# Local attention of an adaLN block: head scores in a two-bank PSUM tile, mask by a product, one maximum, exponentials from PSUM, norms for two chunks at once

## Chip, cores and metric

The kernel runs on one core of one Trainium2 chip. The time is device microseconds (us) of one launch; lower is better. TensorE is called PE, VectorE DVE, ScalarE ACT, GpSimd POOL, and the queue that issues most transfers SP. L965 means line 965 of the kernel before, whose functions are printed below with their line numbers.

## The reference, cut to what matters

The input is x of 16 batches, 512 tokens, 128 features. An attention with latent keys and values (16 heads of 8) comes first, wrapped in adaLN modulation. Then two layers follow, each with a windowed ("local") attention of 8 heads of 64 and a gated MLP. The change touches the local attention:

```
q, k, v = split(shift(x) @ wqkv)                 # 8 heads of 64
q = l2norm(q) * qs ;  k = l2norm(k) * ksc
q, k = rotary_xpos(q, k)
# windows of 64 queries, each against its own 64 keys and the 64 keys before them
sim  = einsum(q * 8, k)
mask = (i < j) | (i > j + 64) | (j == -1)
sim  = where(mask, -max, sim)
out  = einsum(softmax(sim), v)
x    = x + out @ wo
```

## The kernel before

The first attention fills about the first 700 us. Each of the two layers then has a local-attention part (about 715 to 1270 us and 1455 to 2050 us in the profiled execution) and an MLP part after it.

The local attention works in chunks of 128 tokens, that is two windows of 64; there are 4 chunks in each of 16 batches and 2 layers, so 128 chunks. `proj_steps` makes q, k and v of a chunk, `chunk_steps` does its attention, and `out_steps` multiplies by wo once in a batch.

- Projection, `blk(n)`: for each of q, k, v three 512-column matmuls (L877 to L879: high and low parts of the operands) into one PSUM bank `ps_s`. For q and k, ACT squares the bank (L887), DVE multiplies it twice with the rotary tables (L891), DVE sums the squares (L901), POOL adds the two products into `r` (L904). `norm` takes the inverse square root of the 16 sums (L916, two small ACT instructions, L189, L192, L195), stores minus 8 times that of q in `nrq` (L921) and multiplies k by its own on POOL (L923). `tr(j)` transposes r with four PE instructions (L930) and ACT copies the result to qT or kT (L143).
- Scores, `s1(par)`: four heads of one parity (even or odd; they lie in partitions 0-63 or 64-127) go into one bank `ps_e` (L965, a 64x64 piece of the array each). Then for each of the four heads one DVE instruction (L978) adds the mask, multiplies by `nrq`, writes `pr` to SBUF and yields the minimum; one ACT instruction for each head takes the exponential of `pr` and its sum `den` (L161).
- `nrm(par)` divides by the sum (DVE L1005, POOL L1006), `s2(par)` transposes (L1014) and copies to pT (L143), `s3` multiplies by v (L1034), ACT rounds the result to `oh` (L143), DVE keeps the rest in `ol` (L1046). `out_steps` is L817 to L819 and L1066.

The order is not that of the loops. A `Plan` gives every step a due time (`LQ` for the six projection steps, `LC` for the eight steps of a chunk, `UC` the length of a chunk) and emits the steps sorted by it; the compiler then schedules the emitted instructions with a timeline of its own. Each engine runs its list in order.

PSUM has eight banks. In the layers the kernel uses three for `ps_s`, two for `ps_e`, two for `ps_m` and one `ps_x`, which every third request of `third("m")` or `third("e")` takes: transposes, the product with v and the product with wo thus turn through three banks. `FB` sets the number of SBUF buffers of hh, hl, sq, t1, t2, r, pr, pT. The MLP part (`mlp_steps`) uses `ps_s` for its gate and up products and `third("e")` for its two transposes.

## Time and profile before

| | |
|---|---|
| median of 3 runs | 2212.19 us (2210.29 to 2213.22) |
| profiled execution, own time | 2217.06 us |
| its span, first to last instruction | 2215.3 us |
| PE busy | 2019.9 us, 91% |
| DVE busy | 1915.9 us, 86% |
| ACT busy | 1622.7 us, 73% |
| POOL busy | 1234.0 us, 56% |
| mean granted TensorE clock | 0.953 |

The profiled execution took 0.22% longer than the median of the runs. Busy time of an engine is the union of its instructions; matmuls are pipelined and overlap, so the sum of their durations is far above the time PE needs for them, and the distance from one start to the next is the better price. "Idle before" is the time for which the engine stood still ahead of an instruction, with the engine whose result ended the wait.

### The profile page before, as it was taken

The page shows a single profiled execution, that of the slowest core. Times are in us where ns is not written, and L with a number is a line of the kernel's source. Part 1 is how long each engine was busy: PE and PEld are TensorE (multiplying, and loading weights), DVE is VectorE, ACT ScalarE, POOL GpSimd, SP SyncE. Part 2 cuts the span into 40 slices and gives each one's busy share as a digit, 9 for nine tenths or more (in the row PEclk, how much of TensorE's full clock was granted, in tenths as well). Part 3 has the DMA queues.
Part 4 walks back from the last instruction along what each step waited for, and adds up shares of the span by engine and source line. Part 5 has one row for each costly group of instructions (what it writes and reads, how often), then busy time and mean ns, then how long its engine had stood idle before and what let it go on. Part 6 is the DMA issues. An engine that isn't in the chain of part 4 may idle for free.

```text
span 2215.3 us, 55787 instructions
## 1 busy us (share of the span) xinstructions
PE 2019.9 (91%) x20362; PEld 1359.0 (61%) x20362; DVE 1915.9 (86%) x5869; ACT 1622.7 (73%) x4318; POOL 1234.0 (56%) x1500
## 2 busy tenths in 40 slices
PE   5879898989985999999999998889999999999888
PEld 3334444444433777777777766667777777777665
DVE  6767788878855999999999999999899989898898
ACT  2666777777784888888888755577788888887555
POOL 4345455545554766666666644476566666664334
PEclk7788999999996999999999999999899999999999
DMA  4335544454532110111111100020101011111022
GB/s 125 104 120 151 144 137 141 141 148 136 149 87 56 28 35 18 35 25 29 30 23 35 39 11 1 1 41 21 35 19 32 21 25 28 25 28 23 17 56 76
DMA packets 101198, 132.78 MB, mean 60 GB/s; under 512 B 15538, under 2 KB 77500, under 8 KB 98876
## 3 DMA queue, kind: packets, MB, share of 16 engines
q1 hardware_dynamic: 100444, 128.67, 21.8%
q8 instruction: 161, 2.64, 0.5%
q14 instruction: 113, 0.93, 0.1%
q10 hardware_dynamic: 480, 0.54, 0.1%
HBM read 48.43 MB, written 50.86 MB: 45 GB/s over the span
## 4 chain that ended last, share of the span: by engine, by line
PE 47%; DVE 34%; DMA 10%; ACT 4%; issue 3%; SPq 1%; POOL 1%; DVEq 0%; ACTq 0%; POOLq 0%
PE ps_e L965 9%; DVE t L891 5%; PE ps_m L724 4%; DVE pr L978 4%; PE ps_s L877 4%; DMA kst<-kdd 3%; DVE mx L585 3%; PE ps_m L1014 3%; PE ps_m L1034 3%; DVE ss L901 3%; PE ps_s L878 2%; PE ps_s L879 2%; DMA kdd<-kd 2%; PE ps_m L930 2%; DVE pr L1140 2%
## 5 line engine op out<-in xcount | busy, mean ns | idle before, releaser
L585 DVE TENSOR_REDUCE mx<-ps_w 128x2 f32<-128x1024 f32 (+3 forms) x448 | 390.1, 911 | 97.5 <-PE ps_w L575 94.5
L161 ACT ACTIVATE pr<-pr,m 128x128 f32<-128x128 f32 x1024 | 404.0, 402 | 60.1 <-DVE m L978 57.5
L904 POOL TENSOR_TENSOR r<-t,t 128x512 f32<-128x512 f32 x256 | 328.3, 1283 | 195.7 <-DVE t L891 79.4
L1006 POOL TENSOR_TENSOR pr<-pr,den 128x512 f32<-128x512 f32 x256 | 266.9, 1043 | 211.6 <-DVE den L1005 120.2
L161 ACT ACTIVATE pt<-ps_w 128x1024 f32<-128x1024 f32 x320 | 324.3, 1025 | 69.0 <-PE ps_w L664 64.6
L965 PE MATMUL ps_e<-kT,qT 64*64 64x128 f32 (+1 forms) x4608 | 354.6, 272 | 3.6 <-DVE m L978 1.6
L891 DVE TENSOR_TENSOR t<-ps_s,tab 128x512 f32<-128x512 f32 x512 | 328.4, 678 | 16.2 <-ACT sq L887 8.3
L978 DVE CUSTOM_DVE_ANT_0 pr<-ps_e,maskl,nrq 128x128 f32<-128x128 f32 x1024 | 298.7, 341 | 48.2 <-PE ps_e L965 47.6
L965 PEld LDWEIGHTS ps_e<-kT,qT 64*64 64x64 f32 x4608 | 251.5, 135 | 127.3 <-issue 103.6
L675 POOL TENSOR_SCALAR_AFFINE_SELECT pt<-pt 128x256 f32<-128x256 f32 (+1 forms) x448 | 191.5, 442 | 242.5 <-ACT pt L161 237.8
L724 PE MATMUL ps_m<-pt,vau 128*32 128x512 f32 (+3 forms) x2048 | 204.6, 467 | 13.0 <-ACT o L143 12.9
L1145 POOL TENSOR_TENSOR kT<-pr,qT 128x512 fp32r<-128x512 f32 x96 | 123.0, 1290 | 165.9 <-ACT qT L143 157.5
L877 PE MATMUL ps_s<-wqh,hh 128*128 128x512 f32 x384 | 186.9, 487 | 25.3 <-DVE t L891 18.5
L161 ACT ACTIVATION_READ_ACCUMULATOR pr<-pr,m 128x1 f32 x1024 | 201.7, 197 | 0.0
L887 ACT ACTIVATE sq<-ps_s 128x512 f32<-128x512 f32 x256 | 152.5, 597 | 51.1 <-PE ps_s L879 40.5
L565 PE MATMUL ps_w<-kst,qst 48*128 48x512 bf16 (+3 forms) x1024 | 157.7, 315 | 33.2 <-ACT pt L161 11.4
L901 DVE TENSOR_REDUCE ss<-sq 128x8 f32<-128x512 f32 x256 | 171.3, 673 | 0.3 <-ACT sq L887 0.3
L664 PE MATMUL ps_w<-qst,kst 50*128 50x512 bf16 (+3 forms) x1024 | 131.1, 308 | 31.5 <-DVE mx L585 29.6
L878 PE MATMUL ps_s<-wql,hh 128*128 128x512 f32 x384 | 157.0, 409 | 0.0
L879 PE MATMUL ps_s<-wqh,hl 128*128 128x512 f32 x384 | 155.4, 406 | 0.0
L923 POOL TENSOR_TENSOR r<-r,rky 128x512 f32<-128x512 f32 x128 | 133.7, 1045 | 37.3 <-DVE rky L195 30.0
L575 PEld LDWEIGHTS <-idm 64*128 64x128 bf16 x2048 | 107.4, 99 | 65.7 <-issue 35.1
(215 smaller groups left out, 4521.3 us busy)
## 6 DMA issues: line engine op xcount, KB each, us to landing
od<-o SPq DMA_DIRECT2D x64, 256.0 KB
v<-v SPq DMA_DIRECT2D x32, 512.0 KB
qst<-qdd SPq DMA_DIRECT2D x64, 192.0 KB
kst<-kdd SPq DMA_DIRECT2D x64, 192.0 KB
v<-v SPq DMA_DIRECT2D x32, 384.0 KB
qdd<-qd SPq DMA_DIRECT2D x16, 384.0 KB
kdd<-kd SPq DMA_DIRECT2D x16, 384.0 KB
xt<-in_L_attn_x_dram SPq DMA_DIRECT2D x16, 256.0 KB
```

The lines of the kernel that those rows point to most:

```text
L161: ins = nc.scalar.activation(*a, **k)
L585: nc.vector.tensor_reduce(dst, src, AX.X, ALU.max)
L724: mm_ = nc.tensor.matmul(p[32 * hl : 32 * hl + 32, kb * 128 : T], lhsT=va[:, kb, h * 9 : h * 9 + 32], rhs=pts[hl, seg][:, off : off + n], ...
L877: nc.tensor.matmul(p, lhsT=hh[:, cols], rhs=wqh[:, wc], start=True, stop=False)
L878: nc.tensor.matmul(p, lhsT=hh[:, cols], rhs=wql[:, wc], start=False, stop=False)
L879: nc.tensor.matmul(p, lhsT=hl[:, cols], rhs=wqh[:, wc], start=False, stop=True)
L891: nc.vector.tensor_tensor(t, pv, W["tab"][:, n, 2 * j + k, :].unsqueeze(1).to_broadcast([128, LH, LD]), ALU.mult,)
L901: nc.vector.tensor_reduce(loc["ss"][:, j, :], sq, AX.X, ALU.add)
L904: nc.gpsimd.tensor_tensor(r.rearrange("p h (x d) -> p h x d", x=2), t1.rearrange("p h (x d) -> p h x d", x=2), t2.rearrange("p h (x d) -> ...
L965: nc.tensor.matmul(p[64 * w : 64 * w + 64, hp * 128 + o : hp * 128 + o + n], lhsT=s["q"][r0 : r0 + 64, hp, q0 + 64 * w : q0 + 64 * w + 64] ...
L978: nc.vector.tensor_tensor_reduce(pr[:, hp, :], p[:, hp * 128 : (hp + 1) * 128], mk, s["nrq"][:, cc, 2 * hp + par : 2 * hp + par + 1], 3.0e ...
L1006: nc.gpsimd.tensor_tensor(pr, pr, den.unsqueeze(2).to_broadcast([128, 4, 128]), ALU.mult)
```

## The change

- `s1` becomes one step for all eight heads. It takes a tile of two banks (`two_later`, tag e, two such tiles), one bank for each parity. Four matmuls first write the mask into it, each in its own 64x64 piece of the array: an identity block times a mask tile that is now four heads wide. The score matmuls accumulate onto that and go round the four pieces (two windows, two parities).
- One DVE `tensor_reduce` takes the maximum of all eight heads from PSUM. POOL multiplies it by `nrq` to `nb`. The exponentials (`ex(par)`) read PSUM, with scale `rq` and bias `nb`.
- The projection works on pairs of chunks: `norm` runs once for two chunks, POOL makes `nrq` from `rq`, k is scaled in two steps `kn`, and q is transposed ahead of the norm.
- Banks: `ps_s` two instead of three, `ps_e` two double banks, `ps_m` two, and no `ps_x`. `third` is gone: its users take `ps_m`, in the MLP `ps_s`; gate and up share a double bank. `FB` gives r six buffers instead of four and pr four instead of six.

```diff
-LQ = (0.0, 0.33, 0.26, 0.563, 1.705, 1.964)
-LC = (0.149, 0.637, 0.789, 0.944, 1.14, 1.772, 2.3, 2.531)
+LQ = (0.0, 0.33, 0.26, 1.2)
+LN = (0.6, 0.7, 0.9, 1.6, 1.9)
+LC = (0.149, 0.6, 0.85, 0.944, 1.14, 1.5, 1.85, 2.3, 2.531)
...
-FB = (3, 2, 2, 2, 3, 4, 6, 4)
-BK = (3, 2, 2)
+FB = (3, 2, 2, 2, 3, 6, 4, 4)
+BK = (2, 2, 2)
...
-    def third(tag):
-
-        turn[tag] = (turn.get(tag, -1) + 1) % 3
-        return bank("x", 1) if turn[tag] == 2 else bank(tag, BK[1] if tag == "e" else BK[2])
+    def two_later():
+        return later["ps"].tile([128, 2, 512], F32, tag="e", bufs=BK[1], name="ps_e")
...
-        m = const.tile([128, 128], BF, name=f"maskl{int(first)}")
+        m = const.tile([128, 4, 128], BF, name=f"maskl{int(first)}")
...
             def norm():
                 ss = loc["ss"]
                 nc.vector.tensor_scalar(ss, ss, 1.0e-24, None, ALU.max)
-                rk, nwt = rsqrt_steps(pool["wk"], ss, [128, 2, LH], "rk", nc.vector)
+                rk, nwt = rsqrt_steps(pool["wk"], ss, [128, 2, 2, LH], "rk", nc.vector)
                 for f in nwt:
                     f()
-                nc.vector.tensor_scalar(s["nrq"][:, n, :], rk[:, 0, :], -QKS, None, ALU.mult)
-                r = loc["r", 1]
-                nc.gpsimd.tensor_tensor(r, r, rk[:, 1, :].unsqueeze(2).to_broadcast([128, LH, LD]), ALU.mult)
+                nc.vector.tensor_scalar(
+                    s["rq"][:, n0 : n0 + 2].rearrange("p n r h -> p n h r"),
+                    rk[:, :, 0, :].rearrange("p n (h r) -> p n h r", r=2),
+                    QKS, None, ALU.mult,
+                )
+                nc.gpsimd.tensor_scalar(
+                    s["nrq"][:, n0 : n0 + 2], s["rq"][:, n0 : n0 + 2], -1.0, None, ALU.mult
+                )
+                loc["rk"] = rk
+            def kn(n):
+                def f():
+                    r = loc["r", n, 1]
+                    nc.gpsimd.tensor_tensor(
+                        r, r, loc["rk"][:, n - n0, 1, :].unsqueeze(2).to_broadcast([128, LH, LD]), ALU.mult
+                    )
...
-            return [mm(0), mm(1), mm(2), norm, tr(0), tr(1)]
+            steps = []
+            for n in (n0, n0 + 1):
+                steps += [mm(n, 0), mm(n, 1), mm(n, 2), tr(n, 0)]
+            return steps + [norm, kn(n0), kn(n0 + 1), tr(n0, 1), tr(n0 + 1, 1)]
...
-        def s1(par):
+        def s1():
+            p = loc["s"] = two_later()
+            tiles = [(w, par) for w in range(2) for par in range(2)]
+            for w, par in tiles:
+                r0 = 64 * par
+                nc.tensor.matmul(
+                    p[64 * w : 64 * w + 64, par, :],
+                    lhsT=identb[r0 : r0 + 64, r0 : r0 + 64],
+                    rhs=masks[int(cc == 0 and w == 0)][r0 : r0 + 64].rearrange("p h k -> p (h k)"),
+                    start=True, stop=False, skip_group_check=True,
+                )
+            for hp in range(4):
+                for w, par in tiles:
+                    r0 = 64 * par
+                    k0 = q0 + 64 * w - 64
+                    parts = [(0, k0, 128)] if k0 >= 0 else [(0, 0, 64), (64, 0, 64)]
+                    for o, kk, n in parts:
+                        nc.tensor.matmul(
+                            p[64 * w : 64 * w + 64, par, hp * 128 + o : hp * 128 + o + n],
+                            lhsT=s["q"][r0 : r0 + 64, hp, q0 + 64 * w : q0 + 64 * w + 64],
+                            rhs=s["k"][r0 : r0 + 64, hp, kk : kk + n],
+                            start=False, stop=True, skip_group_check=True,
+                        )
+            m = small("m", [128, 2, 4], 3)
+            nc.vector.tensor_reduce(m, p.rearrange("p r (h k) -> p r h k", h=4), AX.X, ALU.max)
+            nb = loc["nb"] = small("nb", [128, 2, 4], 3)
+            nc.gpsimd.tensor_tensor(nb, m, s["nrq"][:, cc], ALU.mult)
+            loc["den"] = small("den", [128, 2, 4], 3)
+        def ex(par):
             def f():
...
-                for hp in range(4):
-
-                    nc.vector.tensor_tensor_reduce(
-                        pr[:, hp, :],
-                        p[:, hp * 128 : (hp + 1) * 128],
-                        mk,
-                        s["nrq"][:, cc, 2 * hp + par : 2 * hp + par + 1],
-                        3.0e38,
-                        ALU.add,
-                        ALU.min,
-                        m[:, hp : hp + 1],
-                    )
+                pr = loc[par] = flat("pr").rearrange("p (h k) -> p h k", h=4)
                 for hp in range(4):
                     act(
                         "exp",
                         pr[:, hp, :],
-                        pr[:, hp, :],
+                        loc["s"][:, par, hp * 128 : (hp + 1) * 128],
                         AF.Exp,
-                        scale=-1.0,
-                        bias=m[:, hp : hp + 1],
-                        accum_out=den[:, hp : hp + 1],
+                        scale=s["rq"][:, cc, par, hp : hp + 1],
+                        bias=loc["nb"][:, par, hp : hp + 1],
+                        accum_out=loc["den"][:, par, hp : hp + 1],
                     )
...
         def f1():
-            p = third("e")
+            p = ps_s()
...
         def gate(i):
             def f():
                 zh, zl = s["zT"]
-                p = ps_s()
+                s["gu"] = two_later()
+                p = s["gu"][:, 0, :]
...
         def up(i):
             def f():
                 zh, zl = s["zT"]
-                p = ps_s()
+                p = s["gu"][:, 1, :]
```

## The prediction, made before the changed kernel ran

> **What bounds the kernel now.** I read the busy rows over the span first, then the table by stretches, the chain of waits, and at last the order of PE's instructions.
>
> ```profile
> PE   5879898989985999999999998889999999999888
> DVE  6767788878855999999999999999899989898898
> ...
> 900.00:1250.00 350.00, 345.47 (x3762) 262.79 (x3761) 339.40 (x1194) 298.14 (x1032) 230.03 (x205) 1.00 0.13 30
> 1600.00:1950.00 350.00, 350.00 (x3550) 254.78 (x3550) 316.21 (x1116) 287.78 (x960) 218.28 (x194) 1.00 0.13 27
> 1300.00:1430.00 130.00, 117.43 (x559) 83.33 (x558) 125.95 (x372) 65.90 (x109) 62.30 (x52) 1.00 0.02 5
> 2100.00:2190.00 90.00, 79.50 (x363) 58.45 (x363) 88.89 (x278) 53.86 (x86) 35.45 (x28) 0.98 0.20 56
> ```
>
> Columns of the table: stretch, length, busy PE, weight loads, DVE, ACT, POOL, then granted clock and DMA. The first two stretches are the local attention of layers 1 and 2, the last two the MLPs. PE is never idle in layer 2 and 1% idle in layer 1, where DVE too is at 97%. The MLPs are DVE's (97 and 99%). The clock is full, so it decides nothing. A chunk has four L891 instructions; the stretches hold 156 and 150, so a chunk takes 350/39 = 8.97 us in layer 1 and 350/37.5 = 9.33 us in layer 2.
>
> What PE does with that time is seen in starts, not in durations:
>
> ```profile
> 902.78 1.09 PE L965 MATMUL ps_e<-kT,qT 64*64 64x128 f32 x16
> 903.80 0.45 PE L1034 MATMUL ps_x<-pT,v 128*64 128x64 f32 x6
> ...
> 914.93 0.66 PE L1014 MATMUL ps_m<-ident,pr 128*128 128x128 f32 x4
> 915.35 0.48 PE L877 MATMUL ps_s<-wqh,hh 128*128 128x512 f32 x1
> ...
> 916.13 0.40 PE L877 MATMUL ps_s<-wqh,hh 128*128 128x512 f32 x1
> 916.36 0.40 PE L878 MATMUL ps_s<-wql,hh 128*128 128x512 f32 x1
> ...
> 1203.88 1.59 PE L965 MATMUL ps_e<-kT,qT 64*64 64x128 f32 x32
> 1205.40 0.50 PE L877 MATMUL ps_s<-wqh,hh 128*128 128x512 f32 x1
> ```
>
> A 512-column matmul takes 0.23 us from start to start, four transposes 0.42. A score step of 16 takes 1.02; one of 4 takes 0.37 elsewhere, so 0.054 each plus the change of shape. Price of a chunk: nine projection matmuls 2.08, transposes of q and k 0.84, of pr 0.84, 32 of L1034 0.93 (1.08 us for 32 with a change), the share of wo 0.69, scores 1.75 (28 of 128 columns at 0.054, 8 of 64 at half): 7.13 us. In the instruction order I count changes between the three shapes (128x128, 64x64, 128x64): 8.27 a chunk in layer 1, 10.1 in layer 2. (8.97 - 7.13)/8.27 and (9.33 - 7.13)/10.1 both give 0.22 us a change. So both layers are PE's, and layer 2 is slower because its order changes shape more often.
>
> **The change on PE.** Inside one L965 step only the two windows alternate: two pieces of the array. In the run of 32 at 1203.88 both parities meet, and it takes 1.52 us where two steps apart take 2.04. The middle of it shows why:
>
> ```profile
> 1203.95:1204.37 0.42, 0.42 (x9) 1.00 0.00 0
> 1204.46:1204.72 0.26, 0.26 (x16) 1.00 0.00 0
> ```
>
> Each count is of instructions in flight, so it stands over the stretch plus one length (0.27 us): 13 and 30 per us. Four pieces run at about twice the rate of two. The changed step goes round all four, so I price a score instruction at 0.027: 0.87 us a chunk, 0.88 less. The added mask matmuls are four of 512 bf16 columns. The nearest row, L565 with 512 columns, is busy 56.9 us in 256, 0.22 each: 0.92 us one after another, 0.3 with their loads if the four pieces run together. I take 0.3, since the scores show four pieces together; the other end costs 0.62 x 128 = 79 us. The base becomes 7.13 - 0.88 + 0.30 = 6.55. In the order of the changed kernel there are 7.34 and 7.77 shape changes a chunk: 1.61 and 1.71. PE needs 8.16 and 8.26 us a chunk: 0.81 and 1.07 less, times 64, is 52 + 68 = 120 us. This holds only if PE never waits.
>
> **The other engines, a chunk.** DVE has 8.70 us busy in layer 1 (339.4/39). L978 goes: 91.65/39 = 2.35. The maximum comes: 1.22, from the row of L585 over 1024 elements of PSUM. The five small norm instructions (83.2 us in the stretch, 2.13) run half as often: -1.07. Left 6.5. ACT has 7.64. The eight exponentials read PSUM; a 512-column copy takes 584 ns from PSUM and 620 from SBUF, so 0.04 each, 0.29; the two norm instructions (0.43) halve: left 7.1. Here the Trainium skill says more ("VectorE: DVE Perf Modes", section on the TRN2 errata): ScalarE pays 172 cycles plus the columns from PSUM, that is 250 ns here, against 402 in the row of L161, which would take 1.2 us off ACT. But that page's SBUF price, 293 ns, already misses the row by 109, so I keep the difference of the rows; the page's would make my allowance for waits below some 0.2 us a chunk smaller, 26 us off the sum. POOL has 5.90 and gets `nb` and half an `nrq` (0.225 each, the nearest row is L626): 6.2. None reaches PE's 8.2; DVE's 2.2 us fewer are worth nothing by themselves, as PE hides them in both layers.
>
> **What the change makes wait.** Banks. `ps_s` goes from three to two, and everything in `ps_m` from three to two. PE waits in order, so a bank that is late holds up whatever follows. With the prices above I sum PE's work in the changed order between the last projection matmul into a bank and the next one into it. Before, the mean is 8.3 us; after, behind a q or k tile, 4.6, a quarter of them under 3.4. What a tile needs: 0.4 for the matmul's end, 0.6 for the square, 1.26 for the two products, some 2.4 with nothing in front of ACT or DVE. In the trace before it may take 4.9:
>
> ```profile
> 902.46 0.39 PE L879 MATMUL ps_s<-wqh,hl 128*128 128x512 f32 x1
> 903.38 0.59 ACT L887 ACTIVATE sq<-ps_s 128x512 f32<-128x512 f32 x1
> 906.11 1.28 DVE L891 TENSOR_TENSOR t<-ps_s,tab 128x512 f32<-128x512 f32 x2
> ```
>
> Summing the shortfall over all 256 such tiles: 43 us if a tile is held for 3.2 us, 103 for 4.0, 160 for 4.4, 244 for 4.9. DVE has more room than before, which shortens it; ACT is at 87% of PE's new period. I take about 3.6 us, and add nothing for `ps_m`, as a wait for one bank covers that for another: 64 us, 0.5 a chunk. Bounds: nothing, and 160.
>
> The rule that speaks against the change is the Trainium skill's "TensorEngine Tiling (Array Packing)", section PSUM Bottleneck: tiles speed up TensorE, not the emptying of PSUM, so the copies may become the bound. Read strictly, with the engines that empty PSUM at their old pace and tiles held as above (4.4), the gain turns into +40 us; by the rows alone it is -120. I stand between, since DVE, which does empty these banks, loses a quarter of its load.
>
> **New waits.** The exponentials wait for `nb`, and `nb` stands in POOL's queue behind a division (L1006, 1.04 us) that waits for the sums of the chunk before. Between the two groups of exponentials ACT has three to five copies of 0.55 us: 1.7 to 2.8 us, against 0.17 + 1.04 + 0.23 plus hand-overs, about 1.7. Covered, barely; without the cover the ACT queue, and the double bank, wait up to 1 us. The two `kn` steps now lie together, 2.1 us of POOL ahead of the next `r`, which frees t1 and t2 for DVE; DVE's new room covers it.
>
> **At nothing.** The larger mask tiles: eight selects and two memsets grow about fourfold, some 3 us at 21 to 25 us on POOL, whose next instruction there waits 8.4 us for ACT. The first attention: the instructions come in the same order. The MLPs: DVE sets them; the two transposes share two banks, but between the end of one normalisation and the next statistics DVE has about 6 us of other work against 0.8 for transposing. SP's transfers are the same ones. If the MLP cover were gone, 0.8 x 32 = 26 us.
>
> **The sum.** 2217 - 120 + 64 = 2161 us for the profiled execution. That one ran 4.9 us above the median of the runs, so 2156.
>
> **The rivals.**
> - *PE's saving arrives in full* (0.15): the banks come free in time. For it: almost no wait of PE on ACT or DVE in the stretches before. Against: those had three banks. 2217 - 120 - 4.9 = 2092.
> - *The two-bank queue decides* (0.25, slower). The place: the first projection matmul of each tile, waiting for DVE's L891. It cancels the gain from a hold of 4.2 us on (0.94 us of waits a chunk). At 4.4 it gives +40: 2252; at 4.9, +124. For it: the hold of 4.9 shown, and PE's in-order waits. Against: tiles were held long because three banks let them be.
> - *The mask matmuls run one after another* (0.08): 79 us back, 2235.
> - *The four pieces don't run together for the scores either*: 0.88 x 128 = 113 us of the 120 are gone, and with the waits it is slower; the stretch of 16 in 0.26 us speaks against it, and I count it within the second rival.
>
> **How the numbers follow.** My case, a chunk at 8.6 to 8.8 us, has 0.52. The measurement tells about 0.2% (4.4 us) from no change. Faster by more: 0.52 + 0.15 less 0.01, 0.66; within it 0.05, from the edges of my case and of the second rival; slower 0.25 + 0.08 less 0.04, 0.29. The range reaches from a little below PE's full saving, 2085, to the second rival's first price, 2250; its worse holds stay outside, some 0.1, and less than 0.1 lies below.
>
> **What would show it.** Right: the score lines on PE start about 0.03 us apart and the mask lines add under 0.4 us a chunk; DVE falls to about 75% in the layers; PE's idle time ahead of the projection matmul shows DVE L891, about 0.5 us a chunk; a chunk takes 8.6 to 8.8 us in both layers; MLP stretches are unchanged. Wrong: PE waits over 0.9 us a chunk, ACT is the engine at 95%, the mask lines take 0.9 us, or the MLPs grow by more than 10 us.

## The result: slower, 2238 us

| | before | after |
|---|---|---|
| median | 2211.24 us (2207.09 to 2213.22, 4 runs) | 2238.21 us (2236.22 to 2241.32, 4 runs) |
| ratio, 95% interval | | 1.0126, 1.0107 to 1.0145 |
| span of the profiled execution | 2215.3 us | 2235.7 us |
| layer 1, a chunk, from the first batch's end to the last one's | 8.87 us | 9.17 us |
| layer 2, the same | 9.30 us | 9.18 us |

The last two rows count 60 chunks between the last addition of `out_steps` (L1089 after) in batch 1 and in batch 16: after, 786.8 to 1336.7 us in layer 1, 1548.1 to 2098.6 in layer 2. The 20.4 us of span lie so: 5.1 up to the first batch of layer 1, 17.7 in layer 1, 2.0 in the MLP between the layers, -7.3 in layer 2, 2.9 behind it.

The forecast was 2156 us, 56 us faster than before; the kernel is 27 us slower. That lies inside the range, but it comes about in another way than any that I gave.

The page of the profile after, PE and DVE in 40 slices, and the table by stretches (length, busy PE, weight loads, DVE, ACT, POOL, clock, DMA):

```profile
PE   5878899989984898988888888778888888988887
DVE  6767888787855687777777889977777778788897
```

```profile
900.00:1250.00 350.00, 311.83 (x3808) 228.09 (x3806) 270.39 (x498) 302.05 (x960) 239.03 (x260) 1.00 0.13 27
1600.00:1950.00 350.00, 312.35 (x3806) 228.14 (x3801) 265.58 (x488) 303.42 (x964) 233.67 (x257) 1.00 0.12 25
1320.00:1450.00 130.00, 105.98 (x462) 75.06 (x461) 124.28 (x345) 58.87 (x96) 56.95 (x47) 1.00 0.02 5
2120.00:2210.00 90.00, 79.29 (x359) 55.48 (x359) 88.29 (x267) 53.08 (x85) 35.79 (x28) 1.00 0.19 53
```

The nines of PE in the layers are now eights: PE is idle for 38 us of 350, 11%, where it was idle for 1% in layer 1 and never in layer 2 before. DVE has fallen to 77 and 76%, ACT stands at 86%, no engine is full. A chunk takes as long in both layers. The MLPs are still DVE's (96 and 98%).

PE's own work did shrink as forecast. PE in the timeline after:

```profile
1006.72 0.41 PE L980 MATMUL ps_e<-maskl,identb 64*64 64x512 bf16 x4
...
1012.65 0.50 PE L878 MATMUL ps_s<-wqh,hh 128*128 128x512 f32 x1 [1.28 <-DVE t L892]
...
1034.75 1.10 PE L995 MATMUL ps_e<-kT,qT 64*64 64x128 f32 x32
```

The four mask matmuls run together, 0.41 us for all with the length of the last one, 0.34 to the start of what follows. The 32 score instructions of a chunk take 1.10 us, again with the length of the last one (0.29) in it, so they start 0.026 us apart. The middle row is one of the waits that took the gain away: 1.28 us in which PE waits for DVE's products ahead of a projection matmul.

All that PE waits for in the first stretch (groups of instructions; after the bar the busy time, the mean of one in ns, then PE's idle time ahead of it and what ended it):

```profile
L878 PE MATMUL ps_s<-wqh,hh 128*128 128x512 f32 x114 | 53.5, 469 | 23.9 <-DVE t L892 13.2 <-ACT v L140 9.1 <-PE ps_m L1057 0.2
...
L1057 PE MATMUL ps_m<-pT,v 128*64 128x64 f32 x1216 | 50.8, 227 | 3.4 <-ACT pT L140 3.3
L1037 PE MATMUL ps_m<-ident,pr 128*128 128x128 f32 x304 | 48.0, 280 | 1.3 <-ACT qT L140 1.3
L944 PE MATMUL ps_m<-ident,r 128*128 128x128 f32 x308 | 48.0, 278 | 9.5 <-DVE ol L1069 4.7 <-POOL r L901 3.4 <-ACT kT L140 1.0
```

114 first projection matmuls are 38 chunks. PE waits 23.9/38 = 0.63 us a chunk for the two projection banks and (3.4 + 1.3 + 9.5)/38 = 0.37 us at the instructions that write `ps_m`: 1.0 us together. The second part is of two kinds. Where a copy of `kT` or `qT`, or `ol`, ends the wait, PE waited for a bank: about 0.19 us a chunk. L1057 multiplies `pT` and L944 transposes `r`, so where ACT's `pT` (3.3 us) or POOL's `r` (3.4) ends it, PE waited for the operand itself: 0.18 us a chunk, which a further bank there would not have saved.

And the instruction that changed most against its forecast, first in the kernel before, then after, in the same stretch:

```profile
L161 ACT ACTIVATE pr<-pr,m 128x128 f32<-128x128 f32 x315 | 124.9, 404 | 18.5 <-DVE m L978 17.9
...
L161 ACT ACTIVATION_READ_ACCUMULATOR pr<-pr,m 128x1 f32 x315 | 62.6, 199 | 0.0
```

```profile
L158 ACT ACTIVATE pr<-ps_e,nb,rq 128x128 f32<-128x128 f32 x305 | 139.0, 490 | 2.9 <-POOL nb L1006 2.9
...
L158 ACT ACTIVATION_READ_ACCUMULATOR pr<-ps_e,nb,rq 128x1 f32 x305 | 71.5, 234 | 0.0
```

The exponential was to become 40 ns shorter by reading PSUM. It takes 490 ns instead of 404. Besides the source, one operand is new: `rq`, the scale, is a column (one number for each partition) where there was the constant -1.0.

### The profile page after: what moved, and what is told of

It is laid out like the page before. It is cut to its first block, busy times and chain, and to the rows that moved or that the text cites. A ratio compares the mean times of both kernels' runs of the same rounds, so it can differ in the third digit from the quotient of the medians.

```text
span 2235.7 us, 54736 instructions
## 1 busy us (share of the span) xinstructions
PE 1912.8 (86%) x20874; PEld 1252.5 (56%) x20874; DVE 1728.9 (77%) x3629; ACT 1658.3 (74%) x4190; POOL 1276.7 (57%) x1692
## 4 chain that ended last, share of the span: by engine, by line
DVE 32%; ACT 16%; PE 13%; issue 4%; POOL 2%; ACTq 0%; DVEq 0%; POOLq 0%
DVE t L892 10%; ACT pr L158 8%; DVE ss L898 4%; PE ps_m L944 2%; DVE ss L913 2%; DVE pr L1164 2%; PE ps_e L995 2%; DVE ys L1089 2%; ACT sq L888 2%; ACT oh L140 2%; PE ps_m L1057 2%; DVE m L1004 1%; PE ps_m L1037 1%; DVE ys L1190 1%; POOL r L901 1%
## 5 line engine op out<-in xcount | busy, mean ns | idle before, releaser
L158 ACT ACTIVATE pr<-ps_e,nb,rq 128x128 f32<-128x128 f32 x1024 | 466.7, 491 | 13.9 <-POOL nb L1006 13.7
L1029 POOL TENSOR_TENSOR pr<-pr,den 128x512 f32<-128x512 f32 x256 | 266.9, 1043 | 180.3 <-DVE den L1028 61.4
L878 PE MATMUL ps_s<-wqh,hh 128*128 128x512 f32 x384 | 182.1, 474 | 93.2 <-DVE t L892 53.1
L158 ACT ACTIVATION_READ_ACCUMULATOR pr<-ps_e,nb,rq 128x1 f32 x1024 | 240.9, 235 | 0.0
L140 ACT COPY pT<-ps_m 128x512 f32<-128x512 f32 x256 | 155.4, 608 | 85.4 <-PE ps_m L1037 82.9
L722 PE MATMUL ps_m<-pt,vau 128*32 128x512 f32 (+3 forms) x2048 | 203.9, 465 | 13.1 <-ACT o L140 13.1
L1004 DVE TENSOR_REDUCE m<-ps_e 128x8 f32<-128x1024 f32 x128 | 155.3, 1213 | 61.4 <-PE ps_e L995 57.5
L944 PE MATMUL ps_m<-ident,r 128*128 128x128 f32 x1024 | 163.8, 284 | 33.5 <-DVE ol L1069 12.8
L563 PE MATMUL ps_w<-kst,qst 48*128 48x512 bf16 (+3 forms) x1024 | 156.8, 314 | 32.7 <-ACT pt L158 11.4
L1057 PE MATMUL ps_m<-pT,v 128*64 128x64 f32 x4096 | 173.4, 229 | 12.6 <-ACT pT L140 9.5
L1057 PEld LDWEIGHTS ps_m<-pT,v 128*64 128x64 f32 x4096 | 143.0, 139 | 66.2 <-issue 18.8
L995 PE MATMUL ps_e<-kT,qT 64*64 64x128 f32 (+1 forms) x4608 | 178.8, 270 | 0.0
L1037 PE MATMUL ps_m<-ident,pr 128*128 128x128 f32 x1024 | 163.6, 283 | 11.6 <-DVE ol L1069 5.7
```

The costliest lines, as they stand in the source:

```text
L140: (nc.scalar.copy, nc.vector.tensor_copy, nc.gpsimd.tensor_copy)[EC[i]](dst, src)
L158: ins = nc.scalar.activation(*a, **k)
L722: mm_ = nc.tensor.matmul(p[32 * hl : 32 * hl + 32, kb * 128 : T], lhsT=va[:, kb, h * 9 : h * 9 + 32], rhs=pts[hl, seg][:, off : off + n], ...
L944: nc.tensor.transpose(p[:, hp * 128 : (hp + 1) * 128], r[:, hp * 128 : (hp + 1) * 128], ident)
L995: nc.tensor.matmul(p[64 * w : 64 * w + 64, par, hp * 128 + o : hp * 128 + o + n], lhsT=s["q"][r0 : r0 + 64, hp, q0 + 64 * w : q0 + 64 * w ...
L1029: nc.gpsimd.tensor_tensor(pr, pr, den.unsqueeze(2).to_broadcast([128, 4, 128]), ALU.mult)
```

## The experiments

Theories at the start: (A) the exponentials have become longer, and ACT's delay holds the banks that PE waits for; (B) two projection banks are too few (my second rival); (C) `ps_m` with two banks is; (D) the paired norms hold POOL. Later (E): the order of the instructions. An edit changes more than it says, as the compiler schedules every engine's instructions anew after each; four runs below therefore hold one kernel's order to the instruction. An edit can also move the clock that TensorE is granted. In the local attention (750 to 1250 and 1600 to 2000 us) that is 1.00 before and after, and 0.99 or 1.00 in the four runs with a held order and in e1, e3, e12 and e18. It is a little lower in e4 (0.98 and 0.99) and e11 (0.98, 1.00), lower in e2 (0.97, 0.95), e5 (0.97, 0.98), e8 (0.96, 0.97), e9 (0.97, 0.98), e10 (0.99, 0.92), e16 (0.96, 0.96), and lowest in e6 and e7 (0.89 to 0.91), where a projection matmul (L877 of e6) takes 445 ns in place of 394. No run separates what the clock cost these from what their edit cost.

Each ratio is to the kernel before, timed on the same chip; the changed kernel stands at 1.0126.

### Banks: e1, e2, e12

The double score bank is cut into single ones, with two maxima instead of one; PSUM's eight banks are then dealt out differently.

```diff
-BK = (2, 2, 2)        # ps_s, ps_e (double), ps_m
+BK = (3, 3, 2)        # e1: three for the projections, three score banks
+BK = (2, 3, 2)        # e2: three for ps_m, by a third() as in the kernel before
+BK = (2, 4, 2)        # e12: as many as the changed kernel, only cut
...
-            p = loc["s"] = two_later()
+            p = loc["s"] = [bank("e", BK[1]) for _ in range(2)]
```

> The changed kernel with the double score bank cut into two single banks, three of them in turn, so that ps_s gets its third bank back (e 3, s 3, m 2); two maxima of four heads instead of one of eight. Bank theory (projection matmuls wait for a ps_s bank that DVE's L892 or ACT's copy still holds): PE's idle time ahead of the projection matmuls falls from about 1 us a chunk to under 0.3, a chunk from 9.2 to about 8.6 us, the whole by some 60 to 75 us to about 2170. ACT theory (exponentials at 0.44 us a start instead of 0.39 and ACT's list in order set the pace): under 20 us less. Its order has 8.6 changes of shape a chunk against 7.5, so PE needs 0.25 us a chunk more, which limits the gain.

> The changed kernel with three single score banks, two ps_s, and transposes and the products with v and wo turning through three banks again (e 3, s 2, m 2 and one x). Bank theory with ps_s as the place: little, under 20 us less, since the waits stand at the projection matmuls. If ps_m is the place: a chunk falls from 9.2 to about 8.6 us and the whole by some 60 us. ACT theory: under 20 us.

> Control for the two runs with a third bank: the score tile is cut into single banks as there (two maxima instead of one, four banks, so the same room), and the projections keep two banks, the transposes two. The run with three projection banks took 2257.6 us. If the third projection bank gave nothing: this run lies within 10 us of it, and the cut alone (more changes of shape in PE's order, 8.6 to 9.1 a chunk against 7.3, at 0.22 us) is what made it slower. If the third bank gave what the two-bank theory says (some 0.5 us a chunk of waits): this run is 40 us or more slower than that one, 2297 or above.

Measured: e1 2257.62 us, 1.0202 (1.018 to 1.0225); e2 2313.87 us, 1.0462 (1.0437 to 1.0487); e12 2239.89 us, 1.0131 (1.0104 to 1.0158). e12 is level with the changed kernel, but by another sum: over the 60 chunks of layer 1 PE is busy 520 us in place of 486 and idle 35 in place of 64. Its order changes shape 9.1 times a chunk in place of 7.3. From there a third projection bank, taken from the scores, makes it 18 us slower. The longest waits of e1 in the first stretch (engine, line, what for, us in total, times, longest):

```profile
DVE den L1029 <- ACT pr L158: 51.9, 37, 2.6
POOL pr L1030 <- PE ps_s L880: 45.2, 10, 4.9
ACT pT L140 <- PE ps_m L1038: 44.1, 37, 1.8
```

As theory B had it, the wait of the projection matmul for DVE's products is gone; 5.8 us of waits for ACT's copy of v are left of 23.9. The time went up all the same: PE is busy 528 us over the 60 chunks of layer 1 (8.7 changes of shape a chunk), and POOL and ACT now wait for it. So B names a wait rightly, but neither B nor C is borne out in the form "one more bank would have saved it": neither deal of the eight banks that I tried was better. As each also took a score bank away and came in another order, they don't say what a ninth bank would be worth.

### The column: e3, e13, e14

e3 gives the exponentials a constant scale. The product of the maximum and the norm becomes the negated maximum, by an `nrq` of -1; the scaling of the scores by q's norm is left out.

```diff
-                        scale=s["rq"][:, cc, par, hp : hp + 1],
+                        scale=1.0,
...
-                    s["nrq"][:, n0 : n0 + 2], s["rq"][:, n0 : n0 + 2], -1.0, None, ALU.mult
+                    s["nrq"][:, n0 : n0 + 2], s["rq"][:, n0 : n0 + 2], 0.0, -1.0, ALU.mult, ALU.add
```

> The changed kernel with the exponential's scale a constant 1 instead of the column rq, and nrq set to -1 so that the exponents stay in range: it leaves the norm of q out of the softmax. If the column as scale is what made the exponential dearer (475 ns against 402): it falls to about 366 ns, the distance of two starts from 0.44 to under 0.39, ACT has 0.4 to 0.6 us a chunk less. ACT theory: the whole falls by 40 to 70 us. Bank theory: by under 20 us, since a bank's hold shrinks only a little. If reading PSUM is what made it dearer: 475 ns stay.

Measured: 2178.45 us, 0.9843 (0.9823 to 0.9864), 60 us less than the changed kernel. The exponential, in the same stretch of layer 1:

```profile
L158 ACT ACTIVATE pr<-ps_e,nb 128x128 f32<-128x128 f32 x320 | 116.0, 395 | 4.7 <-POOL nb L1006 4.7
```

It was 490. But the scheduler had also moved other instructions: counted by starts in the traces, 6% of the positions on ACT and PE and 10% on DVE hold another instruction. So e13 is e3 in the changed kernel's order, and e14 is the changed kernel in e3's order. Both add an ordering edge, no wait, between neighbours of each engine's list:

```diff
+    for each engine's list, taken from the other kernel's program:
+        tc.add_manual_dep(ins, previous.name, NoSync)
```

> The kernel of e3 (the changed kernel with a constant scale of 1.0 in the exponentials and nb = -m, so the scaling by q's norm is left out), but with the order of the changed kernel held on PE, DVE, ACT and POOL to the instruction. If the column's price is the cause: exponentials at about 395 ns and 0.38 us apart instead of 0.44, 8 x 0.06 = 0.4 to 0.5 us a chunk less, 2170 to 2190 us as in e3. If e3's gain came from its other order: 2220 or more.

> The counterpart: the changed kernel unchanged in what it computes, held to the order that e3 had. If the column's price is the cause: exponentials at 490 ns, 2225 to 2250. If the order is: 2180 to 2200.

| | column scale | constant scale | difference |
|---|---|---|---|
| order of the changed kernel | 2238.21, 1.0126 | e13: 2198.93, 0.9934 (0.9913 to 0.9954) | 0.0192, 42 us |
| order of e3 | e14: 2225.75, 1.0061 (1.0041 to 1.0081) | e3: 2178.45, 0.9843 | 0.0218, 48 us |
| difference | 0.0065, 14 us | 0.0091, 20 us | |

The column costs 42 to 48 us in either order, the order 14 to 20 us with either scale. Each ratio's interval is about 0.002 wide to either side, so the column's price is known to some 6 us. My number for e13 (2170 to 2190) was too low by the second part: a third of e3's gain (0.0091 of 0.0283) was its order. And even without the column the kernel would be only 12 us faster than before, not 56. In e13 the remaining waits of PE are:

```profile
L160 ACT ACTIVATE pr<-ps_e,nb 128x128 f32<-128x128 f32 x316 | 114.2, 389 | 2.9 <-POOL nb L1008 2.9
...
L880 PE MATMUL ps_s<-wqh,hh 128*128 128x512 f32 x117 | 54.8, 469 | 20.0 <-DVE t L894 12.0 <-ACT v L142 7.4
...
L946 PE MATMUL ps_m<-ident,r 128*128 128x128 f32 x312 | 48.9, 279 | 6.0 <-DVE ol L1071 3.4 <-ACT kT L142 2.3
```

With 117/3 = 39 chunks that is 20.0/39 = 0.51 us for the projection banks, against 0.63 with the column, and 0.17 at `ps_m` (6.0 and 0.5 in two smaller groups) against 0.37. What goes at `ps_m` is nearly all of the other kind: the waits for `pT` and for POOL's `r`, 0.18 us with the column, are gone, and those for banks stay. The order of e3 shows the same: these two waits are 6.7 us in e14 and 0.2 in e3. So more than half of what the column costs PE in the changed kernel's order is operands that come late when the exponentials are longer, and the rest is banks. The wait for `nb` is the same 2.9 us. A chunk takes 8.88 us in layer 1 and 8.92 in layer 2 (785.5 to 1318.4 and 1526.8 to 2062.1 us), 0.25 to 0.28 less.

### The column put into the kernel before: e5, e15

```diff
+    minus1 = const.tile([128, 1], F32, name="minus1")
+    nc.vector.memset(minus1, -1.0)
...
-                        scale=-1.0,
+                        scale=minus1,
```

> The kernel before, with one thing changed: the exponential's constant scale of -1.0 becomes a column of -1.0 (one number for each partition, in SBUF). The work and its source in SBUF stay. My theory (a scale read from a column costs each exponential about 96 ns): the exponential's mean goes from 402 to about 495 ns, ACT's busy time a chunk from 7.64 to about 8.4 us, its starts from 0.39 to 0.43-0.44 us apart, and the kernel becomes slower by 5 to 40 us, as ACT comes near the 8.97 us of a chunk. The rival (the longer exponential of the changed kernel is due to its source in PSUM, or to other work on PSUM, and not to the column): 402 ns as before, and the time within 0.2%.

> The kernel of e5 (the kernel before with the constant scale of -1.0 read from a column), held to the order of the kernel before on every engine. If the column's price is the cause: exponentials at 495 ns and 20 to 45 us slower than before. If e5's loss came from its other order: within 10 us of before.

Measured: e5 2241.6 us, 1.0136 (1.0112 to 1.0161); e15, in the order of the kernel before, 2225.89 us, 1.0066 (1.0046 to 1.0085). The row of e15:

```profile
L163 ACT ACTIVATE pr<-pr,m,minus 128x128 f32<-128x128 f32 x308 | 151.2, 500 | 14.7 <-DVE m L982 14.0
```

No exponential reads PSUM here, the numbers are the same, and the exponential goes from 404 to 500 ns. So the price is the column's and not PSUM's. In time it is 15 us, less than I expected (20 to 45) and a third of its price in the changed kernel. It falls on layer 1, 9.05 us a chunk in place of 8.87; layer 2, where PE is still never idle in its stretch, has 9.24 in place of 9.30. Half of e5's 30 us was order, or the lower clock that came with it.

What each exponential costs ACT is seen from start to start, four kernels in turn: before (constant, from SBUF), e15 (column, SBUF), after (column, PSUM), e13 (constant, PSUM).

```profile
902.60 0.40 ACT L161 ACTIVATE pr<-pr,m 128x128 f32<-128x128 f32 x1
902.90 0.20 ACT L161 ACTIVATION_READ_ACCUMULATOR pr<-pr,m 128x1 f32 x1
902.99 0.40 ACT L161 ACTIVATE pr<-pr,m 128x128 f32<-128x128 f32 x1
```

```profile
903.16 0.49 ACT L163 ACTIVATE pr<-pr,m,minus 128x128 f32<-128x128 f32 x1
903.55 0.19 ACT L163 ACTIVATION_READ_ACCUMULATOR pr<-pr,m,minus 128x1 f32 x1
903.65 0.49 ACT L163 ACTIVATE pr<-pr,m,minus 128x128 f32<-128x128 f32 x1
```

```profile
1003.42 0.47 ACT L158 ACTIVATE pr<-ps_e,nb,rq 128x128 f32<-128x128 f32 x1
1003.77 0.20 ACT L158 ACTIVATION_READ_ACCUMULATOR pr<-ps_e,nb,rq 128x1 f32 x1
1003.87 0.46 ACT L158 ACTIVATE pr<-ps_e,nb,rq 128x128 f32<-128x128 f32 x1
```

```profile
1001.23 0.37 ACT L160 ACTIVATE pr<-ps_e,nb 128x128 f32<-128x128 f32 x1
1001.49 0.20 ACT L160 ACTIVATION_READ_ACCUMULATOR pr<-ps_e,nb 128x1 f32 x1
1001.58 0.37 ACT L160 ACTIVATE pr<-ps_e,nb 128x128 f32<-128x128 f32 x1
```

In these rows that is 0.39, 0.49, 0.45 and 0.35 us; the medians of all such pairs in the traces are 0.386, 0.479, 0.436 and 0.343. The two effects add up: PSUM as the source takes 0.04 off, as I had put it, and the column puts 0.09 on. Eight a chunk: -0.34 and +0.74 us of ACT.

### The parts that need no column: e4, e16, e8

e4 is the kernel before with one step for the scores of both parities, going round the four pieces; e16 adds the paired norms of the change to it. e8 is the changed kernel with the norms of one chunk at a time.

```diff
 # e4, e16
-        def s1(par):
+        def s1():
+            p = loc["s"] = [bank("e", BK[1]) for _ in range(2)]
+            for hp in range(4):
+                for w in range(2):
+                    for par in range(2):
 # e8
-                steps += [mm(n, 0), mm(n, 1), mm(n, 2), tr(n, 0)]
-            return steps + [norm, kn(n0), kn(n0 + 1), tr(n0, 1), tr(n0 + 1, 1)]
+                steps += [mm(n, 0), mm(n, 1), mm(n, 2), tr(n, 0), norm(n), kn(n), tr(n, 1)]
```

> The kernel before with one part of the change alone: the score matmuls of both parities in one step that goes round the four pieces of the array; mask, minimum, exponentials, norms and all banks as before. PE's price is 7.13 - 0.88 + 6.4 x 0.22 = 7.66 us a chunk, and DVE's 8.4 to 8.7 becomes the bound: layer 1 almost the same (8.87 to about 8.8), layer 2 from 9.3 to about 8.8, the whole 30 to 50 us faster than the kernel before, about 2170. If the two score banks, now taken at once, stall PE instead: no gain or slower.

> The kernel before with the two parts of the change that need no column scale: the scores of both parities in one step (as in e4) and the norms of two chunks at once. Mask, scaling and minimum stay in one pass on DVE, the exponentials keep their constant scale and their source in SBUF. DVE loses 1.07 us a chunk of its 8.7, PE needs 7.7. If the column is what spoilt the change: 8.3 to 8.6 us a chunk, 2125 to 2165, faster than both kernels. If the paired norms themselves hold things up (two multiplications of k one behind the other on POOL): no better than e4, 2195 to 2215.

> The changed kernel with the norms taken for one chunk at a time, as before the change, everything else kept. It gives back the saving in small instructions: DVE +1.07 us a chunk, ACT +0.21, POOL +0.1. If ACT decides: slower than the changed kernel by up to 0.21 us a chunk, 27 us, so 2238 to 2265. If the pairing itself is what holds POOL (two multiplications of k one behind the other ahead of the sums that free t): 2 to 4% faster, 2150 to 2195.

Measured: e4 2205.95 us, 0.996 (0.9944 to 0.9976); e16 2208.73 us, 0.9991 (0.9974 to 1.0009); e8 2308.61 us, 1.0444 (1.042 to 1.0467). Of the 0.88 us a chunk that the joint scores were to save on PE, e4 keeps some 9 us in all, and misses my 30 to 50: DVE is busy for 330 of 350 us in the first stretch, and PE's longest wait is for its products (10.3 us). e16 takes DVE to 310 and is no faster; PE then waits for POOL, at the transposes of k behind the multiplications by its norm:

```profile
PEld ps_m L937 <- POOL r L926: 19.3, 8, 3.3
...
PE ps_m L937 <- POOL r L926: 17.1, 7, 3.1
```

So D has a place there, 17.1 us of waits in the stretch, beside the clock: at 0.96, some 4% of the 326 us that PE is busy, 13 us, are the clock's by my estimate. In the changed kernel undoing the pairing (e8) raises the time by 70 us, far more than the 27 that I gave as the limit. e8 also changes the order and the clock, and no run separates the three; its number shows only that undoing the pairing is no remedy.

### Moving load between the engines: e9, e10, e11, e18

e9 moves the copy of v from ACT to DVE, e10 that of `oh`, e11 both; e18 computes `nb` on DVE instead of POOL.

```diff
-EC = (0, 0, 0, 0, 0, 0, 0, 0, 0, 0, 0, 0, 0)
+EC = (0, 0, 0, 0, 0, 1, 0, 0, 0, 0, 0, 0, 0)     # e9; e10: the eleventh; e11: both
 # e18
-            nc.gpsimd.tensor_tensor(nb, m, s["nrq"][:, cc], ALU.mult)
+            nc.vector.tensor_tensor(nb, m, s["nrq"][:, cc], ALU.mult)
```

> The changed kernel with one copy a chunk moved from ACT to DVE: that of v from its projection bank (0.61 us). Nothing is left out. If ACT decides, as the run with the constant scale says (0.77 us of ACT less a chunk were worth 60 us, 0.61 of each microsecond): 0.61 x 0.61 x 128 = 48 us faster than the changed kernel, 2185 to 2200, so faster than before too. The rival, that the two projection banks and DVE's queue decide: v's bank now stands in DVE's queue, the waits ahead of the projection matmul grow, and the time is 2235 to 2260.

> The changed kernel with another copy of the same size moved instead: that of the attention's output from its bank (oh, 0.62 us a chunk), which DVE's ol then follows on the same engine. It frees a transpose bank and no projection bank. If ACT's total decides: about the same as the run before, 2185 to 2200. If it matters only where ACT's delay holds a projection bank: less than half of that gain, 2215 to 2240.

> Both copies on DVE. ACT falls by 1.23 us a chunk to about 6.8, DVE rises from 7.1 to about 8.4. If ACT alone decided, the gain would be 96 us, 2142; as DVE then is at about 97% of a chunk of 8.7 us, I expect DVE to be the next bound: 2180 to 2210, no better than one copy alone. Below 2165 would say that DVE's load does not matter there.

> The changed kernel with nb computed on DVE, right behind the maximum, instead of on POOL. Nothing is left out. POOL stood 30 us of 350 idle in front of nb, waiting for the maximum, with the sums that free t and the divisions queued behind it; DVE gets one small instruction a chunk (some 0.2 us). If POOL's blocked queue holds the projection banks: 20 to 50 us faster than the changed kernel, 2190 to 2218, about level with the kernel before or a little faster. If not, or if DVE's queue is as bad: 2230 to 2250.

Measured: e9 2293.23 us, 1.0367 (1.0345 to 1.0389); e10 2323.39 us, 1.0505 (1.0481 to 1.0529); e11 2273.05 us, 1.0276 (1.0253 to 1.0298); e18 2254.06 us, 1.0194 (1.0173 to 1.0215). All four missed; e9 to e11 lie above every outcome that I gave. ACT's busy time fell by 0.4 us a chunk in e9 and e10 and by 0.9 in e11, against 0.65 in e3, and the time rose by 55, 85 and 35 us; both copies together cost less than either alone. In e9 PE waits longer for the moved copy of v than it did for it on ACT (9.1 us in the changed kernel), as my rival there had it:

```profile
PE ps_s L878 <- DVE v L140: 15.2, 9, 1.7
```

So A in the form "ACT has too much to do" is not borne out by them, though none tests it alone. What e13 shows is narrower: shorter exponentials, with everything else in its place, are worth 42 us. That it is their place in the chain that counts is argued, from the late operands in PE's rows. In e18 POOL no longer stands in front of `nb`, and stands in front of the divisions instead:

```profile
POOL pr L1029 <- DVE den L1028: 54.6, 29, 5.0
DVE den L1028 <- ACT pr L158: 37.4, 28, 2.6
```

The first of these waits was 16.5 us in the changed kernel. All of e9 to e11 and e18 reorder the queues, and e9 and e10 run at a lower clock, so none of them prices the moved instruction alone.

### The wait for nb: e17

e17 is the changed kernel in its own order; the exponentials take `nrq` as their bias, which is there early, so that none waits for the maximum. The maximum and `nb` are still computed; the subtraction of the maximum is left out.

```diff
-                        bias=loc["nb"][:, par, hp : hp + 1],
+                        bias=s["nrq"][:, cc, par, hp : hp + 1],
```

> The changed kernel in its own order on every engine, but the exponentials take nrq, which is there long before, as their bias instead of nb: the maximum and nb are still computed, and no exponential waits for them (the subtraction of the maximum is left out of the result). The column scale stays. If the new chain from the maximum over POOL's nb to the exponentials is what holds ACT and with it PE: 15 to 40 us faster than the changed kernel, 2198 to 2223. If the chain is covered, as the prediction had it: 2233 to 2243.

Measured: 2229.58 us, 1.0087 (1.006 to 1.0114). That is 9 us below the changed kernel, between the two expectations, and by the two intervals known to some 7 us. The wait at L1057, for `pT`, falls from 3.4 to 1.0 us; PE's wait ahead of the projections doesn't move at all:

```profile
L880 PE MATMUL ps_s<-wqh,hh 128*128 128x512 f32 x114 | 53.5, 469 | 23.9 <-DVE t L894 13.2 <-ACT v L142 9.1
```

The new chain from the maximum by way of POOL to ACT is therefore nearly covered; about 9 us hang on it.

### The norm of q multiplied in: e6, e7

A whole computation without the column: q is multiplied by its norm ahead of its transposes, on DVE (e6) or POOL (e7), and `nb` is the negated maximum. `r` gets a seventh buffer.

```diff
+            def qn(n):
+                def f():
+                    r = loc["r", n, 0]
+                    nc.vector.tensor_tensor(
+                        r, r, loc["rk"][:, n - n0, 0, :].unsqueeze(2).to_broadcast([128, LH, LD]), ALU.mult
+                    )
...
-            return steps + [norm, kn(n0), kn(n0 + 1), tr(n0, 1), tr(n0 + 1, 1)]
+            steps += [norm, qn(n0), kn(n0), qn(n0 + 1), kn(n0 + 1)]
+            return steps + [tr(n0, 0), tr(n0, 1), tr(n0 + 1, 0), tr(n0 + 1, 1)]
```

> The changed kernel with the norm of q multiplied into q on DVE ahead of its transposes, as the norm of k already is on POOL; the exponentials then have a constant scale of 1.0 and nb is the negated maximum. The whole computation is done. If the column scale is what the changed kernel lost by: exponentials at about 395 ns, a chunk at 8.7 to 8.9 us, 2170 to 2195 us, so faster than both kernels, though DVE gets one instruction of 0.65 us a chunk more (from 78 to about 86% busy). If instead the waits for DVE's products decide (the two-bank theory): the added work on DVE holds the two banks longer and the time stays above 2215. A third outcome, that the q transposes, which now wait for the norm, hold up PE: the exponentials are at 395 ns, the waits ahead of L944 (its number may move by a few lines) grow above 0.5 us a chunk, and the time is 2195 to 2230.

> The same as the run before it, with the multiplication of q on POOL instead of DVE (1.04 us a chunk by the row of k's, POOL from about 6.15 to 7.2 of 8.7 us). If the exponentials decide and POOL has room: within 10 us of the run before it. If POOL's queue decides (nb and the divisions stand behind these multiplications, and ACT and DVE wait for them): 10 to 40 us slower than that run.

Measured: e6 2491.19 us, 1.127 (1.1243 to 1.1296); e7 2517.39 us, 1.1388 (1.1365 to 1.1412). The exponentials came down (376 ns in e6), and everything else became late. Two things show in e6: all four tiles of a pair now go through the transposes in one bunch behind the norm, and the multiplication on DVE takes 1504 ns where I had put 650:

```profile
L931 DVE TENSOR_TENSOR r<-r,rky 128x512 f32<-128x512 f32 x30 | 44.0, 1504 | 0.5
L922 POOL TENSOR_TENSOR r<-r,rky 128x512 f32<-128x512 f32 x30 | 38.7, 1312 | 3.7 <-DVE rky L192 3.4 <-DVE den L1027 0.4
```

The third outcome of my expectation, waits behind the norm, came, at a far higher price (2491 us where I had put at most 2230). No run separates the bunching, the long multiplication and the clock (0.91 in this stretch).

## Why the prediction was wrong, step by step

- **What bounds the kernel.** Right. PE was the bound in both layers, and after the change it needs, period less idle in the middle of the layers, 9.17 - 1.00 = 8.17 us a chunk in layer 1 and 9.18 - 0.99 = 8.19 in layer 2. The prediction had 8.16 and 8.26. With its price of a change of shape, taken from two equations in the profile before, the sum came out.
- **Scores and mask on PE.** Right: 26 ns from one score instruction to the next against 27; the four masks in 0.34 to 0.41 us against 0.3. The third rival, masks one after another, did not occur. In the middle of the layers PE's saving is (8.97 - 0.12 of idle - 8.17) + (9.33 - 8.19) = 1.82 us for a chunk of each layer, 64 times: 116 us against 120. Over whole layers it is less (see the sum below).
- **DVE and POOL.** POOL as forecast, 239.03/38 = 6.3 us (6.2). DVE has 270.39/38 = 7.1, 0.6 above the 6.5 expected, though the five small norm instructions did fall to half, from 2.1 to 1.1 us a chunk. The prediction took the time of whole groups out of DVE's busy time, but groups overlap in the profile: in the stretch before they sum to 405 us against 339 busy. That fits the 0.6. At 77% DVE is not what decides.
- **ACT: the step that failed.** The prediction took the exponential for 0.04 us cheaper, from the source alone, and put ACT at 7.1 us a chunk. It never costed the scale, though the diff shows `scale=-1.0` become `scale=s["rq"][...]`. The source's 0.04 was right; the column's 0.09 was missing. ACT has 302.05/38 = 7.9 us, and 284.98/39 = 7.3 in e13. The Trainium skill's figure that I weighed there ("VectorE: DVE Perf Modes", TRN2 errata: 250 ns from PSUM) was further off in the same direction: 389 ns measured with a constant scale, 490 with a column. Both looked at the source and overlooked the other operands. Another page of the skill has them ("ScalarE: Activation LUTs", What ACT_TABLE_LOAD costs, last paragraph): an activation with a bias column takes about 280 ns plus 0.833 ns a column of the tile, and each further column operand some 93 ns more. For 128 that is 387 ns with the constant scale and 480 with the column, and the runs agree (389 and 490). Estimated by that page, the step would have read +0.74 us a chunk for the column beside the -0.29 for the source, ACT at 7.9 us. The column is worth 42 us of time (e13), the largest part of the miss.
- **Waits for the banks.** The allowance was 0.5 us a chunk for the projection banks and nothing for `ps_m`. e13, without the column, has 0.51 for the projection banks: that number was right, and DVE's products are the larger part of it, as said. The nothing for `ps_m` was wrong: 0.17 us a chunk in e13, and 0.37 with the column, half of it for operands that come late, for which the prediction had no term. That a wait for one bank covers that for another is not what PE's rows show; they stand beside each other.
- **The chain over nb.** Called covered, barely; e17 finds 9 us, known to some 7.
- **The MLPs, the first attention, the mask set-up.** Costed at nothing; outside the 60 chunks of each layer the kernel takes 5.1 + 2.0 + 2.9 = 10 us more, with the first chunks of each layer in it. Most of the 5.1 stand before the layer begins: the first attention's last matmul (L724, L722 after) starts at 667.0 us before and 671.1 after, its first score matmul (L565, L563 after) at 35.1 and 37.9. The eight mask selects take 6.5 us of POOL in place of 3.7, and POOL's next instruction starts 2.6 us later, so the wait of 8.4 us did not cover them as the prediction had it. No run tries the masks alone.

The sum again, on the profiled executions, for the 60 chunks of each layer that the first table counts: before, after, e13.

```profile
781.70:1313.90 532.20, 516.82 (x5587) 393.85 (x5586) 511.39 (x1827) 434.54 (x1476) 330.71 (x292) 0.99 0.12 27
1523.30:2081.10 557.80, 544.45 (x5585) 404.42 (x5580) 496.92 (x1819) 443.18 (x1479) 327.21 (x291) 0.98 0.11 25
```

```profile
786.80:1336.70 549.90, 486.27 (x5832) 357.75 (x5830) 427.32 (x873) 463.29 (x1449) 357.59 (x384) 0.99 0.12 27
1548.10:2098.60 550.50, 485.71 (x5802) 356.78 (x5800) 428.01 (x874) 462.17 (x1447) 351.65 (x381) 0.99 0.12 26
```

```profile
785.50:1318.40 532.90, 485.68 (x5832) 357.63 (x5830) 425.99 (x873) 423.99 (x1449) 354.99 (x384) 0.99 0.13 28
1526.80:2062.10 535.30, 486.49 (x5803) 358.44 (x5801) 426.56 (x874) 423.27 (x1447) 349.19 (x381) 0.99 0.12 26
```

In these 120 chunks PE is busy 89 us less than before, and idle for 128 us in place of 29, 100 more; the other stages take 10 more. That is the 20 us of the spans. The forecast, scaled from 128 chunks to 120, was -112 and +60. So of 73 us, the column is 32: e13 has PE busy as long, 972 us, and idle for 96. Another 23 are a saving of PE that was put too high: the prediction took the time of a chunk in the middle of the layers before, 8.97 and 9.33 us, for PE's own work, which over the 60 chunks is 8.61 and 9.07 a chunk. The waits without the column are 7 above the allowance, and 10 lie in the other stages.

The rival that ended on the slower side, two banks for the projections, gave 2252 us, and waits of 1.0 us a chunk are what it asked for (it decides from 0.94 on). But only 0.63 us of them stand at the place that it named, its cause, DVE's products, carries 13.2/38 = 0.35 us, and a third bank did not help in the order that came with it (e1). So its number was near by luck, by way of a different sum. The Trainium skill's rule that speaks against the change ("TensorEngine Tiling (Array Packing)", PSUM Bottleneck: packing the array does not empty PSUM any faster), read strictly, gave +40 us and so the right sign. What it says is seen in the rows in part: PE needs 1.8 us less for two chunks and then waits, for 0.8 of the 1.0 us a chunk, for the engines that read its banks.

The best of the complete kernels is e4, the joint scores alone, at 0.996 of the time before. e3 and e13 are faster, and leave the scaling out. Still open is a way to scale the scores at less than the column's price; e6 and e7 were none.

## What to carry to other kernels

Read every operand of an instruction that a change rewrites, not only its source and size: a constant that becomes a column can cost more than the better source saves. In a kernel in which no engine is full, ask where in the chain an instruction stands before pricing it by its engine's total: some 0.65 us of ACT a chunk were worth 42 us in the exponentials, while 0.4 us moved away with a copy brought nothing, though there DVE's load, the order and the clock changed too. And when the compiler orders the queues anew after each edit, hold the order in the comparison that is to settle a cause; here order alone moved the time by 14 to 20 us.

## What the runs showed of the hardware

- A scale read from a column instead of a constant made a 128x128 exponential on ACT 96 to 101 ns longer (404 to 500 from SBUF, 389 to 490 from PSUM), 0.09 us from start to start in both (medians 0.386 to 0.479 and 0.343 to 0.436). In the prediction that price was missing.
- The same instruction from PSUM starts the next one 0.04 us sooner than from SBUF, with either scale, though the accumulator's read is longer there (199 to 203 against 227 to 234 ns).
- A 128x512 multiplication by a broadcast norm took 1504 ns on DVE, and 1312 ns on POOL in place of 1043 to 1045, in e6, where both engines do such multiplications at the same time: DVE's run from 934.39 to 937.33 us, two in a row, and POOL's from 935.29 to 938.23. The nearest rows of DVE with that shape are 676 to 684 ns, from PSUM. The Trainium skill ("SBUF — State Buffer", Who interferes with whom) has it that a DVE instruction with two inputs in SBUF contends with a GpSimd instruction that reads SBUF; these rows fit that, and no run here tried it alone.
